# Giving the extra-edge groups more steps of the next block's preparation, in a two-layer graph network on one core

## The chip, the cores and the metric

The kernel runs on one core of a Trainium2 chip. The metric is the device time of one execution in microseconds (us). One more execution was recorded by the hardware profiler; durations of single instructions come from that one. Engines: PE is the matrix engine (PEld its weight loads), DVE the vector engine, ACT the scalar engine, POOL the GpSimd engine, SP the engine that only issues DMAs.

## The reference

x is 3327 x 128 (padded to 3328, 26 blocks of 128 rows), adj 3327 x 3327 with about 2% of its entries set. Layer 0 is a graph attention with four heads, layer 1 a graph convolution, both after a layer norm and a ReLU and added to x:

```python
def _gatv2_head(x, A_shape, w1, w2, a, Wlin):
    x1 = x @ w1
    x2 = x @ w2
    E = leaky_relu(x1[:, None, :] + x2[None, :, :], 0.01)
    s = E @ a
    s = tanh(s / 8.0) * 8.0
    s = exp(s) * A_shape
    s = s / sum(s, axis=-1, keepdims=True)
    return leaky_relu(s @ x @ Wlin.T, 0.01)
# layer 0: h = max(layernorm(x), 0);  x = x + concat(heads of h) @ w
# layer 1: h = max(layernorm(x), 0);  A_t = adj + I;  D = row sums of A_t
#          x = x + relu(D^-1/2 A_t D^-1/2 (h @ W.T + b))
```

## The kernel before

The attention is computed on edges alone. The columns of a row are dealt into two classes by position, and each row of a block gets two lists of 32 edges (the regular edges); edges that don't fit go to a common list of extra edges. For each of the 26 blocks there are two halves (hb, 64 rows each), and each half has nine groups m: groups 0 to 7 hold the regular edges, 512 at a time, and group 8 the extra edges, 384 places. Two regular groups share a fetch w of eight gathers.

A gather (L562) is an indirect DMA issued by POOL. It brings, for 128 edges, one table row each: weights of the edge's column (64), features, and the four heads' projections (512). There are two tables, one for each half. Tiles `g` (four buffers of eight gathers) hold regular edges and one tile `ge` the extra ones (three gathers). A gather waits until its buffer is free, that is until the aggregation (L658, or L676 for extra edges) of the edges that lay there before is done on PE.

A group is computed by three functions. `stage_z` transposes the gathered projections on PE (L587) into the PSUM tile `z`; for regular groups DVE takes the maximum with the row's own projection (L599) into `r`, for the extra group PE adds the row's projection with the matmul L590 and ACT applies the ReLU (L596). `stage_r` multiplies with the attention vector (L610). `finish` turns the scores (L618, L627, L630, L633, L638, L640), weights them (L649, or L665 and L667) and aggregates (L658, L676). `close` ends a block's half (L687 to L749).

The next blocks' preparation, `prep(b, k)`, is a generator of 72 steps (NPREP): it writes codes of the nonzero entries (L401, four times a block), takes the largest eight of each segment (L405), transposes the adjacency on PE and stores it by ACT's DMA queue (L355, L357, L360), adds the row sums (L426 on ACT), asks for the adjacency rows of the next block (L342 on SP), draws the lists by repeated maximum (L434, L436, then L457, L460 for the extra edges), and makes the indices and the row's projections (L440 to L543; L505, L514 to L520 and L526, L532 belong here). L572 on SP writes the weight column of a table from the transposed adjacency, once a half.

Everything is one instruction order written out by a loop over the 468 groups (26 x 2 x 9). Between pieces of a group it calls `slot()`: four times in `stage_z` (after each head's transposes and each pair of heads) and twice outside. A slot lets `finish` and `close` go on by one step each, brings the preparation up to the step that is due, and issues the gathers whose buffers are given back. The due step follows from the count of slots:

```python
t = state["slot"] / SLOTP
advance(NPREP * (1 + t + min(1.0, t) * AHEAD))
```

SLOTP was 6 slots for each of the 18 groups of a block, 108. With AHEAD = 0.5 block 0 carries one and a half times the usual steps, and from then on the first half of block b carries the second half of the preparation of block b+1, the second half of block b the first half of that of block b+2. After block 25 come the rest of layer 1 (L873, L937) and the output.

Of the kernel before, what the change touches and what calls it, by code (L numbers as in the profile page):

```python
# [228 lines left out]
def _sparse_layers(tc, nc, x, adj, w1, w2, a, wlin, w, gw, gb, gb_sb, gwT, x_sb, dinv, flag, ident, out):  # L229
# [19 lines left out]
    NG = 9  # L249
# [4 lines left out]
    with ExitStack() as l0:  # L254
# [321 lines left out]
        def stage_z(k, hb, m, slot):  # L576
            n = 4 * P if m < 8 else OVT * P
            arrived(k, hb, m // 2)
            g = k.g[hb, m // 2]
            out = []  # L580
            for hp in range(2):
                z = ps_z.tile([P, 2, BANK], F32, name="z")
                r = pr.tile([P, 2, BANK], F32, name=f"r{hp}")
                for i in range(2):
                    h = 2 * hp + i
                    for q in range(n // P):
                        nc.tensor.matmul(z[:, i, q * P:(q + 1) * P], g[:, m % 2 * 4 + q, PROJ + h * D:PROJ + (h + 1) * D], ident,  # L587
                                         is_transpose=True, start=(q == 0 or m < 8), stop=(m < 8), skip_group_check=True)
                    if m == 8:
                        nc.tensor.matmul(z[:, i, :n], k.x1b[:, h * D:(h + 1) * D], k.oi[:, hb * n:(hb + 1) * n],  # L590
                                         start=False, stop=True, skip_group_check=True)
                    if i == 0:
                        slot()
                slot()
                if m == 8:
                    nc.scalar.activation(r[:, :, :n], z[:, :, :n], AF.Relu)  # L596
                else:
                    r0 = HALF * hb + 32 * (m % 2)
                    nc.vector.tensor_tensor(r.rearrange("p h (i s) -> p h i s", s=16), z.rearrange("p h (i s) -> p h i s", s=16),  # L599
                                            k.x1n[:, 2 * hp:2 * hp + 2, r0:r0 + 32, None].to_broadcast([P, 2, 32, 16]), OP.max)  # L600
                out.append(r)
            return out
# [156 lines left out]
        NCODE = 20  # L759
        NLIST = 42  # L760
        NPREP = 72
        SLOTP = 6 * 2 * NG
        AHEAD = 0.5
        preps = [prep(b, blks[b]) for b in range(NB)]
        queue = deque()
# [1 line left out]
        state = {"slot": 0, "fetched": 0, "g": 4, "ge": 1}  # L767
# [3 lines left out]
        def advance(upto):  # L771

            for b in range(NB):
                while done[b] < NPREP and b * NPREP + done[b] < upto:
                    if next(preps[b], "end") == "end":
                        done[b] = NPREP
                    else:
                        done[b] += 1
                        assert done[b] < NPREP

        def fetch():
            while state["fetched"] < len(fetches):
                b, hb, w = fetches[state["fetched"]]
                kind = "ge" if b < NB and w == NW else "g"
                if state[kind] == 0 or (b < NB and not blks[b].ready):
                    return
                state[kind] -= 1
                if b == NB:
                    strip(pieces[w])
                else:  # L790
                    gather(b, hb, w)
                    if w == LATE and b + hb > 0 and b + hb < NB:
                        queue.append((None, 0, 0, partial(weights, b + hb, 1 - hb)))
                state["fetched"] += 1
# [8 lines left out]
        def trickle():  # L803
            while queue:
                issue()

        def arrived(k, hb, w):

            while any(q[0] is k and q[1:3] == (hb, w) for q in queue):
                issue()  # L810

        def slot():
            state["slot"] += 1
            t = state["slot"] / SLOTP
            for todo in (tails, ends):
                todo[:] = [f for f in todo if next(f, "end") != "end"]
            advance(NPREP * (1 + t + min(1.0, t) * AHEAD))
            fetch()
            trickle()
            if state["early"] is not None and next(state["early"], "end") == "end":  # L820
                state["early"] = None
# [318 lines left out]
        with tc.manual_schedule():  # L1140
            fetch()
            while queue:
                issue()
            rs = {}
            n = len(groups)
            for i in range(-1, n + 1):
                if i + 1 < n:
                    slot()
                if 0 <= i < n:
                    b, hb, m = groups[i]  # L1150
                    if (b, hb, m) == (max(0, NB - 2), 1, 0):
                        state["early"] = begin()
                    rs[i] = stage_z(blks[b], hb, m, slot)
                if 0 <= i - 1 < n:
                    b, hb, m = groups[i - 1]
                    stage_r(blks[b], hb, m, rs.pop(i - 1))
                    if m % 2 or m == NG - 1:
                        ends.append(finish(blks[b], hb, m // 2))
                    slot()
            lay = layer1()  # L1160
            todo = "one"
            while ends or tails or state["early"] is not None:
                slot()
                if todo == "one":
                    todo = next(lay)
            for _ in lay:
                fetch()
                assert not queue
# [60 lines left out]
def kernel(  # L1229
# [26 lines left out]
    gb_sb = const.tile([P, D], F32, name="gb_sb")  # L1256

    _sparse_layers(tc, nc, x, adj, w1, w2, a, wlin, w, gw, gb, gb_sb, gwT, x_sb, dinv, flag, ident, out)


# [46 lines left out]
```

## Time and profile before

| | |
|---|---|
| Time, median of 3 runs | 2532.93 us (2532.48 to 2535.38) |
| Profiled execution | 2536.74 us, of which the span from first to last instruction is 2534.9 us |
| Mean granted PE clock | 0.98 |
| DMA, mean share of 16 engines busy and rate | 331 GB/s; software queue (gathers) 71.0%, hardware queues 19.1% and 7.0% |
| Chain that ended last | PE 35%, DVE 24%, DMA 20%, POOL 11%, issue 7% |
| First gather issued, last gather done on POOL | 67.1 us, 2427.3 us |

Busy time of an engine is the sum of its instructions' durations. "Idle before" is the time for which the engine stood idle just before an instruction, and the name behind the arrow is what ended it; "issue" means that nothing in the profile was waited for. The profiled execution took 3.8 us more than the median of the runs.

### The profile page before, as it was taken

To read this page: it belongs to the slowest core of one execution; us is meant where nothing else is said; L and a number is where in the kernel's file an instruction comes from. 1 tells how busy PE (TensorE), PEld (TensorE's weight loads), DVE (VectorE), ACT (ScalarE), POOL (GpSimd) and SP (SyncE) were. 2 spreads that over 40 slices of the span, in tenths; PEclk is the share of its full clock that TensorE was granted. 3 is DMA by queue.
4 is the path that set the end of the run, shared out by engine and by line. 5 is a ranking of instruction groups with operands and counts; after the bars stand their busy time and mean duration, and the time that the engine had idled before them with its cause. 6 is when DMAs were issued, how large, how long until landed. Compare 5 with 4: busy or idle time off the path is not lost.

```text
span 2534.9 us, 51974 instructions
## 1 busy us (share of the span) xinstructions
PE 2278.9 (90%) x19410; PEld 1586.2 (63%) x19410; DVE 2030.5 (80%) x6260; ACT 704.1 (28%) x1651; POOL 1791.8 (71%) x1873
## 2 busy tenths in 40 slices
PE   6689899988989998989998999999999899999898
PEld 4456666656666666666666666666666667675553
DVE  7678988888788888878888788988988888895433
ACT  4122233223223222322322322232232233222110
POOL 3577777777777777777777777777777777777620
PEclk9789999999999999999999999999999999999999
DMA  9999999999999999999999999999999999999995
GB/s 294 392 338 314 342 353 318 334 351 335 324 339 346 318 328 359 329 319 343 337 312 336 353 311 341 352 329 329 339 346 318 330 360 313 333 322 347 324 336 186
DMA packets 460759, 838.58 MB, mean 331 GB/s; under 512 B 209099, under 2 KB 318165, under 8 KB 457173
## 3 DMA queue, kind: packets, MB, share of 16 engines
q0 software_dynamic: 145600, 640.34, 71.0%
q1 hardware_dynamic: 219396, 140.96, 19.1%
q10 hardware_dynamic: 95504, 53.88, 7.0%
q8 instruction: 156, 2.56, 0.4%
q14 instruction: 103, 0.84, 0.1%
HBM read 765.93 MB, written 113.42 MB: 347 GB/s over the span
## 4 chain that ended last, share of the span: by engine, by line
PE 35%; DVE 24%; DMA 20%; POOL 11%; issue 7%; ACT 1%; SPq 0%; DVEq 0%; POOLq 0%; ACTq 0%
DMA g<-table,idx 13%; DVE r L599 11%; POOL g L562 10%; PE z L587 10%; PE s L610 6%; PE z L590 3%; DMA ge<-table,idxo 3%; PE z L937 2%; DVE cand L405 2%; PE tr L627 2%; PE ag L658 2%; DMA AT_d<-at 2%; PE tr L370 2%; PE tr L505 1%; DVE codes L401 1%
## 5 line engine op out<-in xcount | busy, mean ns | idle before, releaser
L562 POOL DMA_INDIRECT g<-table,idx x1664 | 1616.3, 971 | 568.3 <-issue 442.2
L599 DVE TENSOR_TENSOR r<-z,x1n 128x1024 f32<-128x1024 f32 x832 | 1010.1, 1215 | 65.5 <-PE z L587 63.9
L587 PE MATMUL z<-ident,g 128*128 128x128 f32 x6656 | 922.4, 278 | 151.9 <-DVE r L599 111.7
L587 PEld LDWEIGHTS z<-ident,g 128*128 128x128 f32 x6656 | 743.8, 142 | 366.9 <-DVE r L599 224.2
L610 PE MATMUL s<-r,sel 128*32 128x512 f32 (+1 forms) x3744 | 491.1, 597 | 0.7 <-ACT ssb L618 0.7
L618 ACT COPY ssb<-s 128x512 f32<-128x512 f32 x260 | 146.7, 564 | 524.6 <-PE s L610 522.5
L630 DVE TENSOR_TENSOR sc<-tr,g 128x32 f32<-128x32 f32 x208 | 38.5, 185 | 300.5 <-PE tr L627 300.5
L405 DVE MAX8 cand<-codes 128x8 f32<-128x52 uint16 x1664 | 215.3, 205 | 0.0
L562 POOL DMA_INDIRECT ge<-table,idxo x156 | 152.6, 978 | 47.5 <-issue 38.1
L638 ACT ACTIVATE th<-sc 128x32 f32<-128x32 f32 x260 | 58.3, 224 | 420.9 <-DVE sc L633 418.5
L590 PE MATMUL z<-oi,x1b 128*128 128x384 f32 x416 | 174.1, 501 | 0.0
L658 PEld LDWEIGHTS ag<-g,wt 128*32 128x32 f32 x3328 | 99.0, 110 | 115.3 <-issue 100.8
L357 ACT COPY at<-tr 128x512 f32<-128x512 f32 (+1 forms) x175 | 97.0, 554 | 222.2 <-PE tr L355 198.3
L627 PE MATMUL tr<-ident,ssb 128*128 128x128 f32 x988 | 153.1, 276 | 5.0 <-ACT ssb L618 4.5
L610 PEld LDWEIGHTS s<-r,sel 128*32 128x32 f32 x3744 | 73.9, 108 | 110.5 <-issue 86.4
L587 PEld LDWEIGHTS z<-ident,ge 128*128 128x128 f32 x624 | 81.4, 146 | 94.8 <-issue 28.5
L596 ACT ACTIVATE r<-z 128x768 f32<-128x768 f32 x104 | 84.3, 810 | 201.7 <-PE z L590 201.7
L658 PE MATMUL ag<-g,wt 128*32 128x133 f32 x3328 | 133.4, 278 | 0.0
L587 PE MATMUL z<-ident,ge 128*128 128x128 f32 x624 | 111.7, 283 | 21.1 <-DMA ge<-table,idxo 18.5
L627 PEld LDWEIGHTS tr<-ident,ssb 128*128 128x128 f32 x988 | 114.3, 141 | 15.3 <-ACT ssb L618 14.9
L355 PE MATMUL tr<-ident,adjb 128*128 128x128 f32 x676 | 107.4, 282 | 16.3 <-DMA adjb<-in_adj_dram 10.2
L401 DVE SCALAR_TENSOR_TENSOR codes<-adjb,code 128x832 uint16<-128x832 f32 x104 | 102.3, 1020 | 1.9 <-DMA adjb<-in_adj_dram 1.9
(188 smaller groups left out, 2350.4 us busy)
## 6 DMA issues: line engine op xcount, KB each, us to landing
adjb<-in_adj_dram SPq DMA_DIRECT2D x26, 1664.0 KB
table<-AT_d SPq DMA_DIRECT2D x52, 832.0 KB
AT_d<-at ACTq DMA_DIRECT2D x150, 256.0 KB
g<-table,idx POOLq DMA_INDIRECT x1664
table<-img SPq DMA_DIRECT2D x12, 1312.0 KB
adjb<-AT_d SPq DMA_DIRECT2D x18, 512.0 KB
g<-AT_d SPq DMA_DIRECT2D x7, 1024.0 KB
g<-AT_d ACTq DMA_DIRECT2D x5, 1024.0 KB
```

The source lines that it names most:

```text
L355: nc.tensor.transpose(pt[:, q, :], adjb[:, (j0 + q) * P:(j0 + q + 1) * P], ident)
L357: nc.scalar.copy(at[:, :n, :], pt[:, :n, :])
L401: nc.vector.scalar_tensor_tensor(codes[:, i], adjb[:, c0:c0 + part], 0.0, code[:, c0:c0 + part], op0=OP.not_equal, op1=OP.mult, accum_out= ...
L405: nc.vector.max(cand[:, c, 8:].rearrange("p (r s) -> p r s", s=32)[:, :, sgm % 32], codes.rearrange("p a b -> p (a b)")[:, sgm % 32 * SEG: ...
L562: return nc.gpsimd.indirect_dma_start(out=g[:, t, lo:COLS], out_offset=None, in_=tab, in_offset=bass.IndirectOffsetOnAxis(ap=at[:, t:t + 1 ...
L587: nc.tensor.matmul(z[:, i, q * P:(q + 1) * P], g[:, m % 2 * 4 + q, PROJ + h * D:PROJ + (h + 1) * D], ident, is_transpose=True, start=(q == ...
L590: nc.tensor.matmul(z[:, i, :n], k.x1b[:, h * D:(h + 1) * D], k.oi[:, hb * n:(hb + 1) * n], start=False, stop=True, skip_group_check=True)
L599: nc.vector.tensor_tensor(r.rearrange("p h (i s) -> p h i s", s=16), z.rearrange("p h (i s) -> p h i s", s=16), k.x1n[:, 2 * hp:2 * hp + 2 ...
L610: nc.tensor.matmul(k.s[32 * h:32 * h + 32, :n], sel[:, h, 31 - at:63 - at], rs[h // 2][:, h % 2, :n], start=(at == 0), stop=(at == 1 or m ...
L618: nc.scalar.copy(ssb[:, :nk * P], s[:, :nk * P])
L627: nc.tensor.transpose(pt[:, q, :], ssb[:, q * P:(q + 1) * P], ident)
L658: nc.tensor.matmul(ag[32 * cg:32 * cg + 32, u, :WORK], wt[:, t].rearrange("p h q -> p (h q)"), g[:, t, FEAT:FEAT + WORK], start=(w == 0 an ...
```

## The change

In the extra-edge group (m = NG - 1 = 8) each of the four slots of `stage_z` counts 2.5 instead of 1, and the number of slots to a block is raised by what that adds: 108 + 2 x 4 x 1.5 = 120. So a slot of a regular group stands for 72 / 120 of a step instead of 72 / 108, and one in the extra-edge group's `stage_z` for 2.5 times that. `finish`, `close` and the gathers still go on once a slot.

```diff
@@ stage_z
                     if i == 0:
-                        slot()
-                slot()
+                        slot(MORE if m == NG - 1 else 1)
+                slot(MORE if m == NG - 1 else 1)
                 if m == 8:
                     nc.scalar.activation(r[:, :, :n], z[:, :, :n], AF.Relu)
@@ constants
         NPREP = 72
-        SLOTP = 6 * 2 * NG
+        MORE = 2.5
+        SLOTP = 6 * 2 * NG + 2 * 4 * (MORE - 1)
         AHEAD = 0.5
@@ slot
-        def slot():
-            state["slot"] += 1
+        def slot(part=1):
+            state["slot"] += part
             t = state["slot"] / SLOTP
```

## The prediction

> **What bounds the kernel now.** I read the page first, then cut one block into its groups, then followed the gather queue, because the page names three engines that are all nearly full.
>
> ```profile
> PE 2278.9 (90%) x19410; PEld 1586.2 (63%) x19410; DVE 2030.5 (80%) x6260; ACT 704.1 (28%) x1651; POOL 1791.8 (71%) x1873
> ...
> L562 POOL DMA_INDIRECT g<-table,idx x1664 | 1616.3, 971 | 568.3 <-issue 442.2
> L599 DVE TENSOR_TENSOR r<-z,x1n 128x1024 f32<-128x1024 f32 x832 | 1010.1, 1215 | 65.5 <-PE z L587 63.9
> ```
>
> By busy shares POOL comes third, with a fourth of its time idle. But nearly all of that idle time is "issue": it waits for nothing that the profile shows. The next view is the busy time of each engine in stretches of block 10, cut at the first z transpose of each group (columns: stretch; length, then PE, PEld, DVE, ACT, POOL busy; clock, DMA share, GB/s). The lines are the extra-edge group of the first half, four regular groups of the second half, and the extra-edge group of that half.
>
> ```profile
> 1034.40:1040.00 5.60, 5.60 (x49) 3.36 (x47) 0.60 (x4) 2.76 (x5) 4.18 (x5) 1.00 1.14 315
> ...
> 1043.10:1051.60 8.50, 7.07 (x71) 5.42 (x68) 8.36 (x32) 2.34 (x6) 6.40 (x7) 1.00 1.00 340
> ...
> 1061.00:1065.70 4.70, 4.44 (x53) 3.23 (x49) 4.70 (x24) 2.29 (x6) 3.48 (x5) 1.00 1.01 378
> 1065.70:1070.30 4.60, 3.65 (x33) 2.34 (x29) 4.53 (x20) 3.69 (x5) 3.69 (x4) 1.00 1.07 384
> 1070.30:1074.50 4.20, 3.56 (x41) 2.35 (x41) 4.10 (x12) 0.35 (x1) 3.13 (x4) 1.00 0.98 374
> ...
> 1078.00:1087.30 9.30, 7.41 (x45) 4.17 (x45) 4.03 (x15) 1.98 (x3) 6.96 (x8) 0.82 1.06 362
> ```
>
> Regular groups are full on DVE (8.36 of 8.50, 4.70 of 4.70); the extra-edge group of the first half leaves DVE idle for 5.0 of 5.6 us and is full on PE. So the change puts DVE work where DVE is free. The question is whether the compute engines set the pace. The timeline of POOL says no (columns: start, us, engine, line, operation, count, idle time before it):
>
> ```profile
> 1004.27 0.95 POOL L562 DMA_INDIRECT g<-table,idx  x1 [0.30 <-issue]
> 1005.52 0.95 POOL L562 DMA_INDIRECT g<-table,idx  x1 [0.30 <-issue]
> 1006.77 1.03 POOL L562 DMA_INDIRECT g<-table,idx  x1 [0.30 <-issue]
> 1008.11 0.95 POOL L562 DMA_INDIRECT g<-table,idx  x1 [0.30 <-issue]
> ```
>
> One gather starts every 1.25 us, 0.946 busy (the median) and 0.305 to the next. A block has 2 x (4 x 8 + 3) = 70 gathers, 87.6 us. The stretch from the first gather of block 2 to the first of block 25 is 23 blocks and exactly 1610 gathers (columns as above):
>
> ```profile
> 265.50:2329.40 2063.90, 1893.70 (x16907) 1343.94 (x16906) 1745.96 (x5353) 599.70 (x1420) 1564.98 (x1610) 0.99 0.99 335
> ```
>
> 1610 x 1.251 = 2014 us of 2063.9. Of the other 50 us, 1564.98 - 1610 x 0.946 = 42 us are gathers that ran longer, and 498.9 - 1610 x 0.305 = 8 us are waits. So POOL's queue of gathers runs without a break through these 23 blocks, at 89.7 us a block. In the timeline the first z of a pair of groups comes 10 to 19 us after its first gather was issued, with four buffers of 8 gathers; PE waits for landings ("PE z L587 <- DMA ge" 17.9 us and "<- DMA g" 8.3 us in that stretch). The compute side alone is a little faster: in blocks 1 to 3, when it was behind (issue to use 25.0 us at block 1, 13.9 at block 4), it took 87.7, 87.9 and 86.7 us. The two rates lie 2.3% apart, but the gathers are the slower one.
>
> Where compute does hold the gathers is the start: one wait of POOL for a buffer in block 1.
>
> ```profile
> 189.95 0.95 POOL L562 DMA_INDIRECT g<-table,idx  x1 [0.30 <-issue]
> 195.89 0.94 POOL L562 DMA_INDIRECT g<-table,idx  x1 [4.99 <-PE ag L658]
> ```
>
> **The change part by part.** *Pace of the steps.* A group has six slots. Before, 72 steps on 108 slots are 0.667 a slot: 4 in a regular group, 4 in the extra-edge group. After, 72 on 120: 3.6 in a regular group, and 4 x 1.5 + 2 x 0.6 = 7.2 in the extra one. By the start of the extra group 28.8 steps are done instead of 32; at the end of each half both stand at 36. Nothing is added or removed; the order of POOL's instructions is the same.
>
> *What moves in a steady block.* In the first half, the instructions that reach the extra group are L511, L514, L516, L518 and L520 (0.16 + 0.41 + 0.40 + 0.40 and about 0.2, 1.6 us of DVE), and on PE L526 (2 x 0.614) and L532 (about 0.7), 1.9 us, while L505 (1.54 us in the chain) slides one group later. In the second half about one and a half pairs of L434 and L436 (0.296 + 0.284 + the load, 0.68 a pair), 1.0 us of DVE. DVE-bound groups lose 2.6 us a block; the first extra group, full on PE, grows by 1.9. Net relief of the compute side: 1 to 2.6 us a block. It lands on nothing: the work that hides it is the gather stream, 89.7 against at most 87.4. What is late next is the landing of the same gather; PE and DVE wait there a little longer. Term: 0. If that cover were gone, 24 blocks x 2.6 would be 62 us.
>
> *The start.* Block 0 runs one and a half times the steps (1.0 a slot before, 0.9 after), so 4.8 more steps per half go to the extra groups; its second half took 57.5 us (138.0 to 195.5), with three regular groups full on DVE (5.9, 6.7, 6.1 us). About 3 pairs, 2 us, leave them. But its longest group, 9.3 us, waits on ACT, which waited 5.45 us for a DMA out of L357's buffers and then ran 3 us of L426; these come later by part of a group, and give back some. The 4.69 us wait shrinks by 0 to 4.7; I take 1.5, as the ACT wait is nearer the end of that chain than the DVE saving is. This shifts the whole stream: -1.5 us.
>
> *Gathers that run longer.* They have a cause, which the change moves:
>
> ```profile
> 1058.34 1.02 DVE L401 SCALAR_TENSOR_TENSOR codes<-adjb,code 128x832 uint16<-128x832 f32 x1
> 1058.60 1.58 POOL L562 DMA_INDIRECT g<-table,idx  x1 [0.30 <-issue]
> ```
>
> A gather that starts while L401 runs takes longer by that instruction's rest less about 0.13 us (here 0.63; 49 of the 51 such gathers, 22 us in all). L649, L497, L667 and a few others do the same; L599 never does (728 cases). A gather starts every 1.25 us, so a lone L401 of 1.02 is met with a chance of 0.895 / 1.251 and costs 0.45 when met: 0.32 each. Before, the two L401 of a quarter stand back to back: one hit for both, 0.47 a pair by the same count, 24 us for 52 pairs (22 seen). After, the changed program's order on DVE has an L599 (1.215) between them: a gather held by the first leaves the next start behind the second, so 0.48 a pair. If more stands between, 0.64, or 33 us. The ends: none met, -22; all met in full, 104 x 0.895 = 93, +71. I take 0, by the pair seen, and +-10 for the range, since positions repeat from block to block and so do not average out.
>
> The Trainium skill, "SBUF — State Buffer", section "Who interferes with whom", says that an operation with two SBUF inputs blocks only GpSimd instructions that read SBUF, and infers that a tensor_tensor leaves descriptor writing alone. The trace differs: 71 of the 96 gathers that started under L649, a TENSOR_TENSOR, were longer by 0.18 us on average. By the page's inference L649 would be free to move, by the row its 13 us are at stake; the measurement decides.
>
> *DMAs of moved steps.* The step with L426 comes 3.8 slots later in the second half, about 3 us, and with it the load of the next adjacency rows (L342, SP). On SP's queue the column table of the next half (L572) stands behind that load. Its packets landed 14 to 20 us before the first gather that reads it (block 16: 1553.5 against 1567.9). 3 us are covered by that; if they were not, every later gather would start late. ACT's stores of L360 spread out. Term: 0.
>
> Sum: 2536.7 (the profiled execution, 2534.9 of span and 1.8 around) - 1.5 = 2535.2. The median of the runs is 3.8 lower, 2532.9, so I say **2532 us** with rounding. A measurement of this kernel can tell about 0.2% (5 us) from no change.
>
> **The rivals.** *Faster: relief reaches the end.* For it: DVE full in the regular groups, 24% of the chain. Against: the gather stream. It cannot give more than the stream's slack: the 4.7 us at the start, up to 8 us of small waits, and some of the 42 us if moved L401, L649 and L497 fall between gather starts; 2516 to 2527. Chance 0.27, most of it from the last.
>
> *Slower: more gathers are held under DVE.* Place: L401 in the first regular groups of each second half and about the middle of it. Price: 0.64 instead of 0.47 a pair, +9 us; with all four of a block met at 0.45, 1.8 against 0.92 a block, +21 us; 2541 to 2554. It decides when something more than one L599 stands between the two L401 (1.25 us or more between end and start), or when L401 starts just before a gather does. For it: back to back is the cheapest arrangement of two. Against: in the changed order the next L401 comes right after one L599. Chance 0.28.
>
> *Slower: PE cools down at the extra group.* In 1078.00:1087.30 PE waited 1.6 us for "ge" and the clock fell to 0.82; pairs of L590 took 1.49 instead of 0.81 and the group 9.3 us. A compute side that is early waits there more often. A loss of 4 us puts issue to use at some 17 to 19 us; POOL had to wait only beyond 20. It decides when two such losses come in a row: 5 us for each, 2540. Chance 0.04.
>
> **How the numbers follow.** Within 0.2%: 0.41, own range 2528 to 2538. Faster 0.27, slower 0.28 + 0.04 = 0.32. The range goes to 2519 below (start wait gone and 10 us fewer held gathers) and to 2549 above (16 us more of them), which leaves out about 2 in 10.
>
> **What would show it.** Right: POOL's stretch from block 2 to block 25 still 2064 us within 10, with waits of 8 us; the first extra group longer (about 7.5 us, DVE about 2 us busy instead of 0.6); DVE's share unchanged; PE's waits for g and ge longer. The wait at 195.89 is shorter or gone. Wrong: POOL waits for "PE ag L658" in many blocks (compute sets the pace), or for "DMA table<-AT_d" (the column table is late), or the excess of the gathers' durations leaves 32 to 52 us.

## The result: slower by 0.4%, and what the profile after shows

| | before | changed |
|---|---|---|
| Median, 9 runs each | 2533.2 us (2528.0 to 2539.7) | 2543.4 us (2538.9 to 2554.7) |
| Ratio | | 1.0043, 95% interval 1.0024 to 1.0061 |
| Profiled execution, span | 2536.74, 2534.9 us | 2540.60, 2538.6 us |

The changed kernel is slower by 10 us. That is inside the range, but not what was forecast; it is the price of the second rival (2541 to 2554). The page of the changed kernel, the same rows as before:

```profile
PE 2295.5 (90%) x19410; PEld 1596.7 (63%) x19410; DVE 2037.9 (80%) x6260; ACT 700.5 (28%) x1651; POOL 1805.0 (71%) x1873
...
L562 POOL DMA_INDIRECT g<-table,idx x1664 | 1630.4, 980 | 560.7 <-issue 447.2
...
L599 DVE TENSOR_TENSOR r<-z,x1n 128x1024 f32<-128x1024 f32 x832 | 1009.4, 1214 | 82.1 <-PE z L587 78.7
L610 PE MATMUL s<-r,sel 128*32 128x512 f32 (+1 forms) x3744 | 502.1, 609 | 0.7 <-ACT ssb L618 0.7
```

Two rows differ. The mean gather went from 971 to 980 ns. And L610, which the change does not touch, went from 597 to 609 ns: PE itself ran slower somewhere. Both matter below. The row of L610 before:

```profile
L610 PE MATMUL s<-r,sel 128*32 128x512 f32 (+1 forms) x3744 | 491.1, 597 | 0.7 <-ACT ssb L618 0.7
```

The gather stream first: the stretch from the first gather of block 2 to the first of block 25 (columns: stretch; length, busy time of PE, PEld, DVE, ACT, POOL; granted clock, DMA share, GB/s).

```profile
263.60:2340.40 2076.80, 1910.96 (x16909) 1356.03 (x16908) 1753.41 (x5360) 596.43 (x1421) 1577.70 (x1611) 0.99 0.99 333
```

The stretch took 12.9 us more than before. Its 1610 gathers (the line counts one over the edge) still take 2014 us at 1.251 each. Summed gather by gather, what gathers ran longer rose from 41.9 to 54.6 us, and what POOL waited from 8.5 to 8.7. So POOL's queue still runs without a break, and the whole loss of the stretch lies in gathers that ran longer. PE still waits for landings in this stretch, 22.5 us against 26.2 before, so the gathers and not the compute side set the pace:

```profile
PE z L587 <- DMA g<-table,idx: 17.3, 38, 1.2
PE z L587 <- DMA ge<-table,idxo: 5.2, 2, 2.8
```

Elsewhere the profiled run gained: 0.8 us to the first gather, 1.1 from there to block 2, 5.4 in the last block, where a wait of POOL fell away, and 1.7 in the tail. The sum is +3.9 (3.7 from the spans). The other 6.3 us between the medians have no trace of their own: the profiled run of before was 3.5 us above its median, that of the changed kernel 2.8 below. But the stretch goes with the medians: in all nine kernels of this document that ran on a chip where the kernel before takes 2533 us, the median lies 463 to 469 us above the profiled stretch (469.3 before, 466.6 changed).

The waiting gather at the start, which was idle for 4.99 us before:

```profile
191.34 0.94 POOL L562 DMA_INDIRECT g<-table,idx  x1 [1.53 <-PE ag L658]
```

The stretches of block 10, cut at the same groups as before: the extra-edge group of the first half, four regular groups of the second half, its extra-edge group.

```profile
1034.10:1041.50 7.40, 7.40 (x61) 4.89 (x57) 2.56 (x9) 3.14 (x6) 5.64 (x6) 1.00 1.11 307
1044.60:1051.30 6.70, 5.94 (x63) 4.56 (x60) 6.67 (x22) 1.76 (x5) 5.48 (x5) 1.00 0.92 302
1062.40:1067.50 5.10, 4.65 (x50) 3.45 (x50) 5.10 (x20) 2.47 (x6) 3.87 (x5) 1.00 1.01 353
1067.50:1071.50 4.00, 3.63 (x34) 2.54 (x30) 3.97 (x18) 1.76 (x5) 3.09 (x4) 1.00 1.06 368
1071.50:1076.00 4.50, 3.66 (x41) 2.38 (x41) 4.43 (x16) 2.90 (x3) 3.38 (x4) 1.00 1.00 356
1079.50:1085.10 5.60, 5.60 (x45) 3.20 (x45) 5.00 (x19) 1.95 (x3) 3.19 (x5) 1.00 0.98 391
```

The steps moved as described: the first extra-edge group carries 2.56 us of DVE work instead of 0.60 and takes 7.4 instead of 5.6; the first DVE-full group went from 8.5 to 6.7. In this block the extra-edge group of the second half keeps its full clock, where it had 0.82 before (below 0.9 in 4 of the 23 blocks before, in 1 now).

**Where the held gathers come from.** Of all held time (48.6 us before, 61.9 after, start and end included) L401 holds 22.1 before and 34.6 after; all other kinds together 26.5 and 27.3 (L649 less, L714 more). The timelines of DVE and POOL at the first pair of block 9 (columns: start, us, engine, line) show how a pair can hold twice:

```profile
957.69 1.01 DVE L401 SCALAR_TENSOR_TENSOR codes<-adjb,code 128x832 uint16<-128x832 f32 x1
...
958.63 1.22 DVE L599 TENSOR_TENSOR r<-z,x1n 128x1024 f32<-128x1024 f32 x1
959.76 1.01 DVE L401 SCALAR_TENSOR_TENSOR codes<-adjb,code 128x832 uint16<-128x832 f32 x1
```

```profile
958.41 1.11 POOL L562 DMA_INDIRECT g<-table,idx  x1 [0.30 <-PE s L610]
959.82 1.78 POOL L562 DMA_INDIRECT g<-table,idx  x1 [0.30 <-issue]
```

The first gather is held for the rest of the first L401, less some 0.13 us. So the next gather starts 1.251 - 0.125 = 1.126 us after that L401's end, wherever in it the first one started. The prediction let this start fall behind the second L401, because an L599 of 1.215 us stands between. But in the trace DVE's instructions overlap by about 0.08 us at each end, and the gap from the first L401's end to the second's start is 1.06 us, not 1.215. The next gather so starts 0.06 us into the second L401 and is held for nearly all of it (0.83 us here). Of the 21 first-quarter pairs with this gap, 11 were met twice (15.8 us) and 10 by the second alone (6.4 us). In the second quarter the usual gap is 1.139 us, on the good side by 0.013 us: in only 2 of 20 such pairs did the second L401 hold a gather. The pairs cost 0.67 us each, against 0.42 before and 0.48 in the prediction.

**What the compute side does.** The prediction's second step was wrong, and the gather queue hid it. Cut at the first z of each group, the regular groups 2, 4 and 6 of the first halves (blocks 3 to 23, means) lost 0.76, 0.76 and 1.80 us, 3.3 in all (the prediction had 1.6 of DVE work leave this half), and the extra-edge group grew by 2.00 (1.9 predicted). But group 7 grew from 5.18 to 7.14. Block 9, group 7 and the extra-edge group, before:

```profile
940.00:945.10 5.10, 5.10 (x41) 3.50 (x39) 4.96 (x14) 1.45 (x4) 3.85 (x5) 1.00 0.90 275
945.10:950.80 5.70, 5.70 (x49) 3.46 (x48) 0.67 (x4) 2.80 (x5) 4.21 (x5) 1.00 1.16 305
```

and the same two in the changed kernel, then PE's and DVE's timelines in the first of them:

```profile
937.80:946.30 8.50, 6.92 (x41) 4.61 (x41) 6.57 (x18) 1.17 (x4) 6.67 (x7) 0.75 0.91 249
946.30:955.00 8.70, 8.70 (x61) 5.79 (x57) 1.62 (x6) 3.15 (x6) 6.57 (x8) 0.85 1.09 358
```

```profile
940.91 0.66 PE L587 MATMUL z<-ident,g 128*128 128x128 f32 x4 [1.58 <-DVE dinv L742]
941.41 2.18 PE L505 MATMUL tr<-lists,oi 128*128 128x46 f32 x12
943.37 1.09 PE L587 MATMUL z<-ident,g 128*128 128x128 f32 x4
944.40 1.94 PE L610 MATMUL s<-r,sel 128*32 128x512 f32 x8
```

```profile
938.63 0.16 DVE L333 SCALAR_TENSOR_TENSOR rs<-q,rs 128x2 f32<-128x2 f32 x1
938.71 1.01 DVE L497 SCALAR_TENSOR_TENSOR oi<-code,end,oi 128x768 f32<-128x768 uint16 x1
939.64 1.22 DVE L599 TENSOR_TENSOR r<-z,x1n 128x1024 f32<-128x1024 f32 x1
940.77 0.15 DVE L742 TENSOR_TENSOR dinv<-rs,dv 128x1 f32<-128x1 f32 x1
```

L497 and the L505 that needs it came one group later. There L497 stands on DVE behind the small instructions of `close` and ahead of the L599 that PE's next z waits for. PE idles 1.58 us. (The row names L742, which stands right behind that L599 and ended 0.06 us after it; in 19 of 23 blocks the wait is put down to L599 itself.) In 11 of the 23 groups 7 of blocks 2 to 24 the granted clock then falls: here twelve L505 take 2.18 instead of 1.54 us, and eight L610 1.94 instead of 1.07; in the eleven, 1.54 to 2.27 and 1.76 to 1.94. Those groups take 7.5 to 8.6 us, the others 6.3 to 6.5; before, all 23 took 5.2, with no idle time of PE. Single L610 of over 900 ns went from 32 to 132. So in the first half the change relieves three groups by 3.3 us a block and loads two others with 4.0.

### The profile page after: what moved, and what is told of

Read it like the earlier page. It is cut to its first block, busy times and chain, and to the rows that moved or that the text cites. A ratio compares the mean times of both kernels' runs of the same rounds, so it can differ in the third digit from the quotient of the medians.

```text
span 2538.6 us, 51937 instructions
## 1 busy us (share of the span) xinstructions
PE 2295.5 (90%) x19410; PEld 1596.7 (63%) x19410; DVE 2037.9 (80%) x6260; ACT 700.5 (28%) x1651; POOL 1805.0 (71%) x1873
## 3 DMA queue, kind: packets, MB, share of 16 engines
q8 instruction: 156, 2.56, 0.4%
## 4 chain that ended last, share of the span: by engine, by line
PE 34%; DMA 23%; DVE 18%; POOL 15%; issue 8%; ACT 1%; SPq 1%; DVEq 0%; POOLq 0%; ACTq 0%
DMA g<-table,idx 15%; POOL g L562 12%; PE z L587 11%; DVE r L599 9%; PE s L610 6%; POOL ge L562 3%; DMA ge<-table,idxo 3%; PE z L590 3%; PE ag L676 2%; PE tr L627 2%; DVE codes L401 2%; DMA adjb<-AT_d 2%; PE ag L658 1%; PE tr L370 1%; DVE cand L405 1%
## 5 line engine op out<-in xcount | busy, mean ns | idle before, releaser
L587 PE MATMUL z<-ident,g 128*128 128x128 f32 x6656 | 940.4, 279 | 155.3 <-DVE r L599 108.1
L599 DVE TENSOR_TENSOR r<-z,x1n 128x1024 f32<-128x1024 f32 x832 | 1009.4, 1214 | 82.1 <-PE z L587 78.7
L610 PE MATMUL s<-r,sel 128*32 128x512 f32 (+1 forms) x3744 | 502.1, 609 | 0.7 <-ACT ssb L618 0.7
L405 DVE MAX8 cand<-codes 128x8 f32<-128x52 uint16 x1664 | 220.0, 202 | 0.0
L658 PEld LDWEIGHTS ag<-g,wt 128*32 128x32 f32 x3328 | 99.4, 111 | 115.2 <-issue 86.6
L658 PE MATMUL ag<-g,wt 128*32 128x133 f32 x3328 | 134.1, 279 | 0.0
L610 PEld LDWEIGHTS s<-r,sel 128*32 128x32 f32 x3744 | 74.4, 109 | 88.5 <-issue 78.3
L355 PE MATMUL tr<-ident,adjb 128*128 128x128 f32 x676 | 108.9, 282 | 15.8 <-DMA adjb<-in_adj_dram 10.3
L355 PEld LDWEIGHTS tr<-ident,adjb 128*128 128x128 f32 x676 | 78.4, 144 | 47.8 <-issue 17.9
```

The source lines that it names most:

```text
L355: nc.tensor.transpose(pt[:, q, :], adjb[:, (j0 + q) * P:(j0 + q + 1) * P], ident)
L405: nc.vector.max(cand[:, c, 8:].rearrange("p (r s) -> p r s", s=32)[:, :, sgm % 32], codes.rearrange("p a b -> p (a b)")[:, sgm % 32 * SEG: ...
L610: nc.tensor.matmul(k.s[32 * h:32 * h + 32, :n], sel[:, h, 31 - at:63 - at], rs[h // 2][:, h % 2, :n], start=(at == 0), stop=(at == 1 or m ...
L658: nc.tensor.matmul(ag[32 * cg:32 * cg + 32, u, :WORK], wt[:, t].rearrange("p h q -> p (h q)"), g[:, t, FEAT:FEAT + WORK], start=(w == 0 an ...
```

## The experiments

Theory A: the gather queue sets the pace, and the loss is gathers held longer. Rival D: the compute side sets the pace and got slower. Rival P: the pair of L401 alone is the cause. "Held" and "waits" below are sums over the gathers of the stretch from block 2 to block 25, from each profiled run; before has 41.9 and 8.5, the changed kernel 54.6 and 8.7. Unless said otherwise, ratios are to runs of the kernel before on the same chip, where its median was 2533. The expectations call theory A also A2 or "gathers held"; B is that the new places of the steps on PE and ACT cost the time, C that the adjacency rows are loaded later.

**e1_pair: the changed kernel, both L401 of a quarter in one step again.**

```diff
                                                        accum_out=csum[...])
-                        yield
+                    yield
+                    yield
```

> The changed kernel with the two L401 of a quarter back to back again (both are issued in one step of the preparation, and two empty steps follow, so that the number and pace of the steps are those of the change). Theory A (gathers held under L401 set the loss): gathers that start under L401 lose 20 to 27 us in all instead of 34.6, POOL's stretch from block 2 to block 25 is back at about 2064 us, and the time at 2528 to 2536 us. Theory B (the loss comes from the new places of the steps on PE and ACT, and PE's clock): 2540 to 2548 us, as with the change. Theory C (the later load of the adjacency rows): also 2540 to 2548.

Measured 2544.3 us, ratio 1.0040 (1.0022 to 1.0058): no gain, and not the 2528 to 2536 of theory A. The profiled execution was the slowest of twelve, 10.6 us above the median. L401's hold fell as expected, from 34.6 to 26.8 us over the run, but the other kinds took back 6 (60.3 in all, against 61.9), and waits rose to 13.3. Rival P falls: undoing the pair alone gives nothing back.

**e2_apart: the kernel before, the second L401 one step later.**

```diff
-                        yield
+                        if i == 0:
+                            yield
+                            yield
```

> The kernel before, with its even pace of 108 slots, but with the second L401 of a quarter one step later, so that an L599 stands between the two. Nothing else of the change is in it. Theory A: L401 holds the gathers for 30 to 38 us instead of 22, and the time rises by 8 to 15 us, to 2541 to 2548. Theories B and C: within 4 us of before.

Measured 2543.9, ratio 1.0037 (1.0021 to 1.0054), held 52.4, waits 11.7. The time is as theory A expected, the way is not: L401 held 21.9, no more than in the kernel before, while L649 (14.9) and L497 (10.1) held more. Moving one step shifts everything behind it against the beat of 1.25 us. Theories B and C expected no loss here.

**e3_dve: the changed kernel with eight more MAX8 of 52 columns a block**, which hold no gather (in the changed kernel none of the 188 that started under L405's was longer).

```diff
+                if m < 8:
+                    more = pb.tile([P, 8], mybir.dt.uint16, name="more", bufs=1)
+                    nc.vector.max(more, code[:, :SEG])
```

> The changed kernel with eight more MAX8 of 52 elements a block on DVE, 0.2 us each, one in every second regular group; their result is not used. They have one input in SBUF and hold no gather. Theory A (the gather stream sets the pace): 1.6 us more DVE a block are hidden, 2538 to 2550 us, POOL's waits for buffers stay under 15 us. Theory D (after the change the compute side sets the pace): 24 x 1.6 = 38 us more, about 2580 us.

Measured 2541.8, ratio 1.0026 (1.0006 to 1.0046), no slower than the changed kernel. Rival D in its plain form falls: 1.6 us of DVE time a block added to the changed kernel would have cost 38 us. Waits rose to 12.0, though.

**e4_small: the changed kernel, each L401 cut in four** of 208 columns.

```diff
-  nc.vector.scalar_tensor_tensor(codes[:, i], adjb[:, c0:c0 + part], ...)
+  for u in range(4):
+      ...
+      nc.vector.scalar_tensor_tensor(codes[:, i, o:o + part // 4], adjb[:, at_u:at_u + part // 4], ...)
```

> The changed kernel with each L401 cut into four of 208 columns. A held gather then waits for the rest of about 0.3 us instead of 1.02. DVE has about 0.9 us more a block. Theory A: the gathers lose under 10 us to L401 instead of 34.6, time 2510 to 2522 us. Theories B, C: 2540 to 2550 us; theory D: 2555 to 2570 us.

Measured 2537.7, ratio 1.0019 (1.0002 to 1.0036). L401's hold fell from 34.6 to 8.0, but the time by 6 us only, not to the 2510 to 2522 of theory A. All other kinds together held 37.7 (27.3 in the changed kernel), 10.3 of it L714, and waits rose to 16.2; seven waits for "PE ag", the long ones in block 17 and later, make 8.8 of them (5.9 in the changed kernel). Something else was close behind.

**e6d_cut_after and e7d_cut_before: both kernels, with L401, L440, L497 and L714 each cut in four.** The two differ from each other only by the change itself.

> The changed kernel with L401, L440, L497 and L714 each cut in four instructions of a quarter of their width, so that the longest rest under which a gather can be held is about a quarter. Theory 'gathers held under two-input DVE instructions': holds plus waits in the stretch from block 2 to block 25 fall from 63 us to 20 to 35 us, and the time falls with it to 2505 to 2525 us. Theory 'the compute side sets the pace': the extra DVE instructions are paid in full, 2545 us or more.

> The kernel before with the same four instructions cut in four. Theory 'gathers held': the holds fall from 49 us to about 16 to 25 us and the time from 2533 to 2500 to 2518 us, within 6 us of the cut version of the changed kernel, because the difference between the two kernels was one of holds. Theory 'compute': 2535 us or more.

| | uncut | cut in four |
|---|---|---|
| kernel before | 2533.2 | 2510.7, ratio 0.9915 (0.9891 to 0.9938) |
| changed kernel | 2543.4 | 2554.8, ratio 1.0095 (1.0071 to 1.0118) |

On the kernel before, theory A's numbers came out: the stretch fell by 16.4 us, held to 20.2, and the time by 22.5 us. This version beats both kernels. On the changed kernel theory A fails and rival D is right: 2554.8 instead of 2505 to 2525, holds plus waits 73 us instead of 20 to 35. The two cut versions were to end within 6 us of each other, as their difference "was one of holds"; they lie 44 us apart. The stretches of e6d and e7d:

```profile
258.80:2345.30 2086.50, 1912.17 (x16900) 1358.19 (x16898) 1789.16 (x6094) 596.14 (x1421) 1551.06 (x1610) 0.98 0.98 331
```

```profile
259.90:2307.40 2047.50, 1886.64 (x16897) 1345.22 (x16895) 1784.90 (x6086) 599.37 (x1420) 1543.25 (x1610) 0.99 0.99 337
```

Held fell in e6d too, by 26.6 us to 28.0, but POOL's waits rose by 36.3 to 45.0. Who was waited for, in e6d:

```profile
POOL g L570 <- issue: 384.2, 1251, 1.3
POOL g L570 <- PE ag L666: 42.5, 20, 4.8
```

The answer is for 263.6 to 2340.4 us (columns: in all, times, longest). L666 is the cut kernels' L658: gathers waited for buffers that PE had not given back. In neither cut version did PE wait for the landing of a gather in blocks 1 to 24, so their blocks show the compute side's own pace: 89.0 us a block with the old placement and 90.7 with the new, and in blocks 14 to 23 89.3 and 91.9. The same instructions, placed anew, cost 1.7 us a block more. (In e7d, too, the gathers alone would take 2034 us, 88.4 a block: with the holds cut, PE's side sets the last of its pace.) In blocks 15 to 23, by groups: groups 2, 4 and 6 of the first half lose 2.8 us, group 7 grows from 5.49 to 8.07, the extra-edge group from 5.62 to 7.80; the second half is longer by 0.6. Group 7 of block 17 in e6d, then in e7d:

```profile
1657.80:1667.50 9.70, 7.69 (x41) 5.46 (x41) 6.96 (x21) 1.14 (x4) 7.26 (x9) 0.69 1.08 284
```

```profile
1643.40:1648.80 5.40, 5.33 (x42) 3.50 (x39) 5.23 (x15) 1.44 (x4) 4.18 (x5) 1.00 1.09 270
```

```profile
1661.34 1.01 PE L595 MATMUL z<-ident,g 128*128 128x128 f32 x4 [1.97 <-DVE r L607]
1662.15 2.63 PE L513 MATMUL tr<-lists,oi 128*128 128x46 f32 x12
...
1665.60 1.94 PE L618 MATMUL s<-r,sel 128*32 128x512 f32 x8
```

It is the wait of the uncut kernel's group 7, 0.4 us longer because four pieces of L497 (L505 here) take 1.40 us, and again the granted clock falls, to 0.69 over the group; 16 of 23 groups were hit. The cuts themselves add 46.4 us of DVE time to the kernel before and 42.9 to the changed one, 1.79 and 1.65 us a block. With all of that taken off, an estimate for the uncut compute side is 87.2 us a block with the old placement and 89.0 with the new, which is within 1.3 us of the 90.3 of the changed kernel's gathers. So a gain from fewer holds has little room in the changed kernel. In e1 and e4 that limit was only part of it: other holds grew by 6 and 10 us in place of those of L401, and waits by 4.6 and 7.5.

**e8d_shift: the kernel before with AHEAD = 0.53**, nothing given to the extra-edge groups. One L599 comes between the two L401 of nearly every second-quarter pair.

```diff
-        AHEAD = 0.5
+        AHEAD = 0.53
```

> The kernel before with AHEAD 0.53 in place of its own value, so that one L599 stands between the two L401 in about half of the pairs. Theory 'held gathers, each placement a draw': holds plus waits of 55 to 68 us in the stretch, and 2538 to 2550 us. Theory 'only the extra group matters': 2533 us within 3 us, since no step goes to the extra edges' groups.

Measured 2550.4, ratio 1.0064 (1.0046 to 1.0082): held 58.8, waits 10.2, L401 alone 37.6 over the run. In the second quarter 10 of 23 pairs with the gap under 1.126 us were met twice (12.8 us); but the first quarter's pairs, back to back, were met by the second in 21 cases (16.0 us). The other theory expected 2533 within 3 us. So a shift of steps without the change's own placement makes the same loss by held gathers. And back to back is not cheap in itself: it was cheap in the kernel before because gathers happened to start early in the pair.

**Runs that tell nothing of the time.** On four other chips the kernel before itself took 3232 to 3319 us (medians), with hundreds of microseconds in which PE and DVE stood idle on "issue" or "remote", without an event of this program; POOL waited over 750 us there in the stretch, against 8.5, so the ratios are of a different bottleneck. They were e5_small_before (the kernel before with only L401 cut: 1.032), e6_cut_after (1.053, repeated 1.053), e7_cut_before (1.037, repeated 1.032 and 1.032), e8_shift (1.069, repeated 1.071 and 1.078), and the two runs that were to read the compute side's pace with the queue out of the way. These bring the wrong rows for one regular edge in eight, so their output is not that of the reference:

```diff
                 lo = 16 * (t // 2) if w < NW else 0
+                if b >= 2 and w < NW and t == WT - 1:
+                    return nc.sync.dma_start(g[:, t, lo:COLS], tables[hb][:P, lo:COLS])
```

> The kernel before, with the eighth gather of every regular fetch from block 2 on replaced by a plain DMA of the same 128 rows' worth of bytes from SP (its rows are not the wanted ones, so one part in eight of the regular edges is left out; 0.001 is added to the sums before L687, one small DVE instruction a half). POOL then issues 62 gathers a block, 77.6 us instead of 87.6, so the compute side sets the pace and can be read directly: no waits of PE for landings, waits of POOL for the aggregation in every block. Every theory: 87 to 88 us a block in blocks 2 to 24, stretch 2000 to 2025 us, time 2465 to 2495 us.

> The changed kernel with the same replacement. Theory 'the change relieves the compute side' (the prediction's step, 1 to 2.6 us a block): 23 to 60 us less than the same replacement on the kernel before, 85 to 86.5 us a block. Theory 'the change slows the compute side' (from the cut versions, whose last blocks took 91.9 us on the changed kernel and 89.3 on the one before, less about 1.6 us of added DVE work): 88.5 to 90.3 us a block, 23 to 60 us more, time 2500 to 2540 us.

Measured 3119.7 (ratio 0.939) and 3116.0 (0.941), 113.0 and 112.4 us a block: 22 us a block or more above anything that either theory expected, and no difference. The direct reading of the uncut compute paces therefore stays open. What such a chip could still show is the holds, which are counted gather by gather: 20 to 21 us of held time in the cut versions of the changed kernel, 16 to 17 in those of the kernel before, 47 to 58 with AHEAD 0.53, in the same order as later.

> The kernel before with each L401 cut into four of 208 columns, the partner of the run with the same cut in the changed kernel (2537.7 us). Theory A2 (the gather queue sets the pace, and what DVE holds it plus what it waits decides; the change reshuffled these): L401 holds the gathers for 5 to 9 us instead of 22, some of it comes back by other instructions in new places; 2522 to 2536 us, and the sum of held time and waits from block 2 to block 25 tells the time to within 6 us. Theory B (the places of the steps on PE and ACT): 10 us under the cut changed kernel, whatever the held time.

> The changed kernel with L401, L440, L497 and L714 each cut into four pieces, so that a gather which starts under one of them waits for a quarter of it at most. DVE has about 1.6 us more a block. Theory A2: held time 28 to 38 us instead of 62, time 2518 to 2532 us. Theory B: no less than the 2537.7 us of the run with L401 alone cut.

> The same four cuts in the kernel before. Theory A2: with little left to hold, the two schedules come together: within 5 us of the changed kernel with the same cuts, or slower than it if DVE's 1.6 us more a block make the compute side the limit of the even schedule (87.4 + 1.6 = 89.0 against 88 to 89 of the gathers). Theory B: about 10 us faster than the changed kernel with the same cuts.

> The kernel before with AHEAD = 0.53 instead of 0.5: all steps come 2.2 steps earlier from block 1 on, at the even pace, and nothing is favoured beside the extra edges. An L599 then stands between the two L401 in half of the pairs. Theory A2: a reshuffle like any other; L401 holds 25 to 32 us, time 2535 to 2546 us. Theory B (steps beside the extra edges cost) and C (a later load; here it comes earlier): 2530 to 2536 us.

## Why the prediction was wrong, step by step

- **What bounds it: right.** POOL's waits are 8.5 and 8.7 us in the two kernels, and PE waits 26.2 and 22.5 us for landings (that this wait would grow did not come true). e7d shows it by experiment: less holding, less time. The sum itself gives 2531.4, where 2532 was said.
- **"Gathers that run longer ... I take 0": the term that failed.** It was +12.7 us in the stretch. The count of one lone L401 and the price of 0.64 for a pair held up; the placement did not: "a gather held by the first leaves the next start behind the second" is off by 0.07 us, since the gap is 1.06 us and the next start comes at 1.126. The rival's condition, "1.25 us or more between end and start", was off in the same way: after a hit on the first the costly gap is anything under 1.126 us that leaves more than 0.125 us of the second L401, so from about 0.23 us on. The mechanism and the price were the second rival's, given 0.28.
- **"Net relief of the compute side: 1 to 2.6 us": wrong in sign.** The two terms that were priced have the right sign and about the right size (groups 2, 4, 6 and the extra-edge group). Left at nothing was "L505 slides one group later": DVE's L497 came ahead of an L599 in group 7, and PE waited for both. On the cut pair the compute side is 1.7 us a block slower, not faster. In the changed kernel's stretch it cost nothing, since 90.3 us of gathers a block cover it and POOL waited no longer; it does cost as soon as the gathers get quicker. The first rival, "relief reaches the end", is refuted: there is none, and the fewer held gathers that it also counted on came as more.
- **"PE cools down" (0.04): right in kind, wrong in place.** Not the landing of ge but a wait of 1.6 to 2.0 us in group 7 comes before the lower clock. Hidden in the changed kernel, it is part of e6d's loss. No run takes L497 alone back to its old place, so the share of this wait is read from the groups and not tested.
- **The start: -1.5 predicted, -1.9 measured** to block 2. The wait shrank by 3.5 us where 1.5 was said, the first gather came 0.8 earlier, and 1.9 came back in the second half of block 1, so the number is close by luck.
- **Loads: right.** From block 2 on L572's packets land at least 11 us before the first gather that reads them (at least 13 before), and no gather waited for them.
- **On the Trainium skill.** "SBUF — State Buffer", section "Who interferes with whom", infers that a tensor_tensor does not stop descriptor writing. In the changed kernel, too, 32 of the 55 gathers that started under L649 were held, by 0.20 us on average. The prediction took such a row to contradict the page. It shows the hold, but not which part of the gather is held: a gather also reads its `idx` tile, and by the same section a GpSimd instruction that reads SBUF does contend. "TensorE: Matmul & The Clock Gate", "Part 1: The HAM clock gate", gives an idle window of about 3.4 us for the clock to fall to half. Here a visible idle time of 1.58 us was followed by matmuls at about half rate (1.94 against 1.07 us) in 11 of the 19 groups 7 that had it, so here a shorter gap was not safe.

**What stays open.** Why e1 and e2 moved the holds to just those other instructions is not predicted by anything here; each placement is a new set of phases between DVE's order and a beat of 1.25 us. An estimate by chance alone: 24 us for the pairs back to back or 33 for pairs apart, by the prediction's count, and some 30 for the other holding instructions (for each, its duration less 0.125, squared, over 2 x 1.251); 54 and 63 in all. By it the kernel before (48.6) was a favourable case and the changed one (61.9) an ordinary one.

## What to carry to other kernels

When a queue of equal instructions sets the pace, price a move by where its instructions fall against that queue's beat, and use measured gaps between starts and ends, not the sum of durations in between. When a step is moved, price the group it lands in as well as the one it leaves, above all if it comes ahead of an instruction that another engine waits for. A bottleneck within 2% of the next one gives gains only as far as that one: here cutting the holding instructions in four was worth 22 us with one placement and cost 11 with the other.

## What the runs showed of the hardware

- A gather that starts under a DVE instruction such as L401 ends 0.82 us after that instruction does (0.946 less 0.125), and the next one starts 0.305 later: from there the beat of the queue is set anew by DVE. Below 0.125 us of rest nothing is held.
- A wait of the same 1.58 us in the same group was followed by a lower PE clock in 11 of 19 blocks and not in the other 8; what tells them apart is not shown.
- The kernel before took 2533 us on three occasions and 3232 to 3319 on five others, and in the kernels traced on those the difference is idle time of PE, DVE, ACT and POOL alike.
